# Graph attention: self-loops added to the sums by VectorE from rows by head and node, and the one-hot scaling folded into the weights

## The chip, the cores and the metric

The kernel runs on one core of a Trainium2 chip. The metric is the device time of one execution in microseconds (us). The median of three runs is shown beside the lowest and the highest. One more execution was taken by the hardware profiler, and every row of the profile comes from that one.

## The reference, cut to what matters

Four graph layers follow each other on 6,250 nodes with 128 features and 106,250 edges. The edges are sorted by destination. The change touches only the fourth layer, an attention with H = 3 heads in which each node also attends to itself over a "loop" edge:

```
row2 = concat([row, loop]); col2 = concat([col, loop])
ea2  = concat([edge_attr, loop_attr])          # loop_attr: mean of the node's edge attributes
alpha = a_src[row2] + a_dst[col2] + a_edge
alpha = where(alpha >= 0, alpha, 0.2 * alpha)
m = segment_max(alpha, col2)
ex = exp(alpha - m[col2])
denom = segment_sum(ex, col2)
attn = ex / denom[col2]
agg = segment_sum(attn[:, :, None] * xp[row2], col2)
y = agg.reshape(n, H * OUT) @ lin_W + lin_b
return layernorm(x + y) * ln_g + ln_b
```

So for each node and head there is a maximum over the logits of the node's edges and of its own loop, then a sum of exponentials, and a sum of source rows weighted by them.

## The kernel before, in words

**The stages ahead of it.** Sums of edge features, a graph convolution and two more neighbour sums fill the first 2,310 us of the span. The last of them, in the function `then` (L1000 to L1032), normalises the node features x, and writes one row of XW = 136 numbers for each node to the DRAM table x3: 128 features, 3 source logits, the number 1, 3 loop logits, and padding. ScalarE's queue sends these rows (L1032), and a memset on GpSimd sets the ones (L1006).

**The attention loop.** The edges are cut into 208 blocks of 512 (BT = 4 tiles of 128 edges). Because edges are sorted, the destinations of a block lie in a window of BW = 40 nodes; where it starts is held in a table, from which SyncE and VectorE load registers, four blocks at a time (`bases`, L296 to L310). The last tile of the block before also counts as one, so that a node whose edges cross a block's border is whole. With the loops, S = BT + 2 = 6 tiles are worked on for each block: the tile carried over, four own tiles, and a tile of the window's nodes, one node in a row, for the loops. A stage `relb` (L146 to L152) holds for each edge the position of its destination in the window; the loops' column in it is simply the row number (L151).

Three functions do the work of a block b:

- `weigh(b)` (L1082 to L1118): GpSimd gathers four tiles of source rows from x3 (L1087), SyncE loads the window's 128 rows for the loops (L1093). VectorE makes logits z for the four own tiles (L1095, then `lrelu`, L312), ScalarE copies the loops' logits (L1097) and those of the tile carried over (L1099). VectorE compares positions with 0 to 39 (L1103: a one-hot of 128 x 6 x 40), turns 1 and 0 into 0 and -1e30 (L1108), and adds z for the three heads (L1110: 128 x 720). TensorE transposes the six parts, each 128 x 120, into PSUM (L1115), and VectorE takes the maximum over all edges (L1118): one number for each of 120 pairs of head and node.
- `power(b)` (L1120 to L1127): TensorE transposes the maxima back, copied over 128 rows (L1122), VectorE subtracts them (L1125), ScalarE takes the exponential (L1127).
- `gather(b)` (L1129 to L1143): six fp32 matmuls sum the rows and the ones, weighted (L1136: 120 x 132; each is two records in the profile, while a transpose is one). VectorE takes the reciprocal of the denominator (L1138), ScalarE scales (L1140), TensorE transposes (L1142), and VectorE copies the result to its window in `acc` (L1143).

**What sets the order.** The loop at the function's end calls power(b - 1), gather(b - 2) and weigh(b), and after every 16 blocks or so `end` (L1064 to L1080), which multiplies `acc` with the output weights (L1069) and does two layernorms. A scheduler then orders the instructions of each engine ahead of time; each engine works through its own queue in that order. Waits are on semaphores. Pools set how far work runs ahead: 8 buffers of gathered rows, 5 of loop rows, 4 of z, 3 each of one-hots and weights, 2 PSUM tiles of two banks each for the transposes, 2 for the sums.

```python
        for b in range(NBT + 2):
            if 1 <= b <= NBT:
                power(b - 1)
            if b >= 2:
                gather(b - 2)
            if b < NBT:
                weigh(b)
```

Of the kernel before, what the change touches and what calls it, by code (L numbers as in the profile page):

```python
# [8 lines left out]
F32 = mybir.dt.float32  # L9
I32 = mybir.dt.int32  # L10
AF = mybir.ActivationFunctionType
OP = mybir.AluOpType
AX = mybir.AxisListType
# [6 lines left out]
F = 128  # L20
# [5 lines left out]
H = 3  # L26
EPS = 1e-5
LOW = -1e30
# [12 lines left out]
BT, NBT, BW = 4, 208, 40  # L41
PB, NB5 = 125, 50
# [8 lines left out]
XW = 136  # L51
# [3 lines left out]
def gnn_kernel(ctx: ExitStack, tc: tile.TileContext, a: dict, out: bass.AP):  # L55
    nc = tc.nc
    const = ctx.enter_context(tc.tile_pool(name="base", bufs=1))
# [4 lines left out]
    part = const.tile([128, 1], F32, name="part")  # L62
# [15 lines left out]
        "relb": const.tile([128, NBT, BT + 2], F32, name="relb"),  # L78
# [4 lines left out]
    with tc.tile_pool(name="ix", bufs=1) as sp, \  # L83
# [51 lines left out]
        for c in range(0, NT, 417):  # L135
            w = min(417, NT - c)
# [14 lines left out]
        nc.vector.tensor_copy(relb[:, :, BT + 1:BT + 2].rearrange("p g j -> p (g j)"),  # L151
                              part.to_broadcast([128, NBT]))  # L152
# [49 lines left out]
def by_windows(ctx: ExitStack, tc: tile.TileContext, a: dict, out: bass.AP, consts, ix):  # L202


    nc = tc.nc
# [785 lines left out]
    with tc.tile_pool(name="l2bw", bufs=2) as work, \  # L991
# [8 lines left out]
        def then(k):  # L1000
# [5 lines left out]
            nc.gpsimd.memset(xw[:, :, F + H:XW], 1.0)  # L1006
# [13 lines left out]
            nc.vector.tensor_copy(xw[:PB, :nb, F:F + H], ap[:PB, :nb, 0:H])  # L1020
# [5 lines left out]
            nc.vector.tensor_add(lg, lg, xw[:PB, :nb, F:F + H])  # L1026
# [24 lines left out]
    S = BT + 2  # L1051
    with tc.tile_pool(name="gb", bufs=8) as gp, tc.tile_pool(name="lr", bufs=5) as lrp, \
# [29 lines left out]
        def weigh(b):  # L1082
# [9 lines left out]
            loop = loops_[b] = lrp.tile([128, XW], F32, name="loop")  # L1092
            nc.sync.dma_start(loop, x3[ds(of_sp(b), 128), :])  # L1093
            z = zs[b] = zbp.tile([128, S, H], F32, name="z")
            nc.vector.tensor_add(z[:, 1:1 + BT, :], r[:, :, F:F + H], zed[:, BT * b:BT * (b + 1), :])  # L1095
            lrelu(z[:, 1:1 + BT, :].rearrange("p j h -> p (j h)"))
            nc.scalar.copy(z[:, S - 1, :], loop[:, F + H + 1:F + 2 * H + 1])  # L1097
            if b:
                nc.scalar.copy(z[:, 0, :], zs.pop(b - 1)[:, BT, :])  # L1099
            else:  # L1100
# [5 lines left out]
                                    op=OP.is_equal)  # L1106

            nc.vector.tensor_scalar(oh, oh, -1.0, -LOW, op0=OP.add, op1=OP.mult)  # L1108
            w = ws[b] = wbp.tile([128, S, H, BW], F32, name="w3")
            nc.vector.tensor_tensor(w, oh.to_broadcast([128, S, H, BW]),  # L1110
                                    z.rearrange("p j (h w) -> p j h w", w=1).to_broadcast([128, S, H, BW]),
                                    op=OP.add)
            tp = tps.tile([H * BW, 2, 512], F32, name="w_p")
            for j in range(S):
                nc.tensor.transpose(tp[:, j // 3, j % 3 * 128:(j % 3 + 1) * 128],  # L1115
                                    w[:, j, :, :].rearrange("p h w -> p (h w)"), ident)
            mx = ms[b] = zbp.tile([H * BW, 1], F32, name="mx")
            nc.vector.tensor_reduce(mx, tp[:, :, 0:384], AX.XY, OP.max)  # L1118

        def power(b):  # L1120
            mb = both[:, b % 2]
            nc.tensor.transpose(mb.rearrange("p h w -> p (h w)"), ms.pop(b).to_broadcast([H * BW, 128]),  # L1122
                                ident[:H * BW, :H * BW])
            wf = ws[b].rearrange("p j h w -> p j (h w)")
            nc.vector.tensor_tensor(wf, wf, mb.rearrange("p (j h) w -> p j (h w)", j=1)  # L1125
                                    .to_broadcast([128, S, H * BW]), op=OP.subtract)
            nc.scalar.activation(wf, wf, AF.Exp)  # L1127

        def gather(b):  # L1129
            wf = ws.pop(b).rearrange("p j h w -> p j (h w)")  # L1130
            loop = loops_.pop(b)
            r0 = rows.pop(b - 1)[:, BT - 1, 0:F + H + 1] if b else loop[:, 0:F + H + 1]
            o = ops.tile([H * BW, F + H + 1], F32, name="o")
            for j in range(S):
                rr = r0 if j == 0 else loop[:, 0:F + H + 1] if j == S - 1 else rows[b][:, j - 1, 0:F + H + 1]
                nc.tensor.matmul(o, lhsT=wf[:, j, :], rhs=rr, start=(j == 0), stop=(j == S - 1))  # L1136
            rd = zbp.tile([H * BW, 1], F32, name="rd")
            nc.vector.reciprocal(rd, o[:, F + H:F + H + 1])  # L1138
            on = obp.tile([H * BW, F], F32, name="on")
            nc.scalar.activation(on, o[:, 0:F], AF.Copy, scale=rd)  # L1140
# [707 lines left out]
```

## Time and profile before

| what | value |
|---|---|
| median of three runs | 3670.23 us (3645.24 to 3673.68) |
| the profiled execution's own time | 3699.71 us |
| its span, first to last instruction | 3697.9 us, 43585 instructions |
| first loop row load (the attention loop begins) | 2309.97 us |
| attention loop to the end of the span | 1388 us, 6.67 us for each of 208 blocks |
| TensorE, matmuls busy over the span | 2650.3 us (72%) |
| VectorE busy | 1841.0 us (50%) |
| ScalarE busy | 911.8 us (25%) |
| GpSimd busy | 1651.7 us (45%) |
| mean granted TensorE clock | 0.803 of full |

A row of instruction groups has the line, the engine, the operation, what it writes and reads with shapes, how often, the busy time and the mean of one in ns, and then the idle time of the engine just ahead of these instructions with what ended it. PE is TensorE, PEld its weight load, DVE VectorE, ACT ScalarE, POOL GpSimd, and a name with a q at its end is that engine's sequencer. A matmul's end is modelled, not measured. "issue" and "remote" name waits for which no instruction is seen that ended them.

### The profile page before, as it was taken

What the parts mean: (1) busy time and instruction counts of PE and PEld (TensorE: products, weight loads), DVE (VectorE), ACT (ScalarE), POOL (GpSimd) and SP (SyncE); (2) the same over time, 40 slices, a digit from 0 to 9 for tenths busy, and PEclk for the clock granted to TensorE, in tenths of its full rate; (3) what the DMA queues carried; (4) which work ended last, traced back from release to release, by engine and by line L of the source; (5) the groups of instructions that cost most, each with busy time, mean ns of one, the idle gap of its engine ahead of it and who ended that gap; (6) DMA issues with size and microseconds to landing.
All of it is one profiled execution on the core that took longest, in us unless ns stands there. A gap on an engine that the chain in (4) does not pass through costs nothing.

```text
span 3697.9 us, 43585 instructions
## 1 busy us (share of the span) xinstructions
PE 2650.3 (72%) x14544; PEld 1631.1 (44%) x14544; DVE 1841.0 (50%) x6113; ACT 911.8 (25%) x1657; POOL 1651.7 (45%) x1684
## 2 busy tenths in 40 slices
PE   2787879776689859999787894465556666555665
PEld 1334436332234424445333442355555555545555
DVE  4899975455522630000211123465666666566666
ACT  0677764200000510001100010122222222222222
POOL 3000010366660575440555521665656656665662
PEclk6677779798889979999887996677777767777777
DMA  5588851465555346653554562222222222222221
GB/s 156 177 280 274 281 195 48 124 194 160 159 168 177 79 116 195 199 181 113 160 170 144 174 173 69 58 53 57 58 58 56 59 57 56 54 59 55 57 56 34
DMA packets 333524, 461.85 MB, mean 125 GB/s; under 512 B 43998, under 2 KB 217854, under 8 KB 332933
## 3 DMA queue, kind: packets, MB, share of 16 engines
q1 hardware_dynamic: 250754, 278.98, 25.5%
q0 software_dynamic: 54912, 105.86, 11.6%
q10 hardware_dynamic: 27624, 74.14, 5.4%
q8 instruction: 117, 1.92, 0.2%
q14 instruction: 117, 0.96, 0.1%
HBM read 375.30 MB, written 83.36 MB: 124 GB/s over the span
## 4 chain that ended last, share of the span: by engine, by line
PE 42%; issue 12%; DVE 11%; another core or an unknown queue 5%; DMA 3%; POOL 2%; ACT 2%; DVEq 1%; SPq 0%; ACTq 0%; POOLq 0%
PE sums L812 21%; PE o L1136 10%; PE w_p L1115 4%; DVE w L1125 2%; DVE w L1110 1%; POOL row L767 1%; PE both L320 1%; PE yp L981 1%; ACT w L1127 1%; DVE mx L1118 1%; PE both L1122 1%; PE fp L1069 1%; PE hp L869 1%; PE both L1142 1%
## 5 line engine op out<-in xcount | busy, mean ns | idle before, releaser
L812 PE MATMUL sums<-piece,arena 125*128 125x500 bf16 x4500 | 1051.3, 387 | 61.1 <-issue 47.2
L1087 POOL DMA_INDIRECT rows<-x,srca x831 | 821.0, 988 | 552.6 <-issue 212.1
L767 POOL DMA_INDIRECT row<-table,srca x549 | 540.0, 984 | 436.0 <-issue 138.8
L812 PEld LDWEIGHTS <-arena 125*128 125x128 bf16 x4500 | 439.1, 99 | 610.9 <-issue 148.8
L1136 PE MATMUL o<-rows,w 128*120 128x132 f32 x2078 | 446.1, 368 | 252.0 <-issue 137.4
L1136 PEld LDWEIGHTS o<-rows,w 128*120 128x120 f32 x2078 | 382.9, 258 | 297.5 <-issue 167.5
L614 ACT CAST arena<-made 128x1000 bf16<-128x1000 f32 (+1 forms) x260 | 312.8, 1261 | 63.6 <-PE made L612 55.3
L611 DVE TENSOR_SCALAR okey<-iok,key 128x250 bf16<-128x250 bf16 x1000 | 314.5, 314 | 0.0
L1115 PE MATMUL w_p<-ident,w 128*120 128x128 f32 x1248 | 246.0, 341 | 92.7 <-DVE w L1110 45.7
L1127 ACT ACTIVATE w<-w 128x720 f32<-128x720 f32 x208 | 167.0, 803 | 532.5 <-DVE w L1125 380.9
L612 PE MATMUL made<-okey,olow 128*128 128x250 bf16 x1000 | 249.7, 331 | 61.7 <-ACT arena L614 27.5
L609 DVE TENSOR_SCALAR olow<-iob,low 128x128 bf16<-128x128 bf16 x1000 | 279.6, 280 | 0.0
L1125 DVE TENSOR_TENSOR w<-w,both 128x720 f32<-128x720 f32 x208 | 187.5, 901 | 178.7 <-remote 106.3
L1118 DVE TENSOR_REDUCE mx<-w_p 120x1 f32<-120x768 f32 x208 | 198.2, 954 | 156.1 <-PE o L1136 85.9
L1115 PEld LDWEIGHTS w_p<-ident,w 128*120 128x120 f32 x1248 | 198.0, 177 | 112.1 <-issue 89.1
L322 ACT COPY by_node<-both 128x128 f32<-128x128 f32 (+1 forms) x48 | 12.7, 264 | 896.1 <-PE both L320 630.8
L331 DVE TENSOR_TENSOR onehot<-iota,relg 128x384 f32<-128x384 f32 x118 | 65.9, 561 | 258.5 <-remote 115.2
L612 PEld LDWEIGHTS <-olow 128*128 128x128 bf16 x1000 | 108.6, 114 | 184.9 <-DVE okey L611 87.3
L1110 DVE TENSOR_TENSOR w<-oh,z 128x720 f32<-128x720 f32 x208 | 186.8, 898 | 0.2
L683 POOL MEMSET ea<- 128x128 f32 x1 | 0.2, 228 | 397.5 <-PE sums L320 397.5
L320 PE MATMUL both<-row,onehot 128*32 128x128 f32 x1098 | 65.6, 312 | 141.3 <-DVE arena L327 94.0
L1142 PE MATMUL both<-ident,on 120*128 120x120 f32 x208 | 71.6, 344 | 111.8 <-DVE w L1125 85.7
(283 smaller groups left out, 3196.2 us busy)
## 6 DMA issues: line engine op xcount, KB each, us to landing
piece<-edges SPq DMA_DIRECT2D x300, 625.0 KB
edges<-arena ACTq DMA_DIRECT2D x100, 625.0 KB
ea<-in_edge_attr_dram SPq DMA_DIRECT2D x69, 768.0 KB
loop<-x SPq DMA_DIRECT2D x208, 68.0 KB
rows<-x,srca POOLq DMA_INDIRECT x831
row<-table,srca POOLq DMA_INDIRECT x549
eat<-in_edge_attr_dram POOLq DMA_DIRECT2D x28, 236.0 KB
table<-xn SPq DMA_DIRECT2D x24, 250.0 KB
```

The source lines that it names most:

```text
L609: nc.vector.tensor_scalar(o, iob, low[:, g:g + 1], None, op0=OP.is_equal)
L611: nc.vector.tensor_scalar(w, iok, key[:, g:g + 1], None, op0=OP.is_equal)
L612: nc.tensor.matmul(p[:, i, 0:NB5 * GD], lhsT=o, rhs=w, start=True, stop=True)
L614: nc.scalar.copy(to, p[:, 0:n, 0:NB5 * GD].rearrange("p i (h d) -> p i h d", d=GD))
L767: nc.gpsimd.indirect_dma_start(out=r[:, j, :], out_offset=None, in_=table, in_offset=bass.IndirectOffsetOnAxis(ap=ix["src"][:, t:t + 1], a ...
L812: nc.tensor.matmul(p, lhsT=xp[:PB, h, i, :], rhs=t[:PB, :, (h - h0) * SC:(h - h0 + 1) * SC], start=(h == 0 and i == 0), stop=(h == NB5 - 1 ...
L1087: nc.gpsimd.indirect_dma_start(out=r[:, j, :], out_offset=None, in_=x3, in_offset=bass.IndirectOffsetOnAxis(ap=ix["src"][:, BT * b + j:BT ...
L1110: nc.vector.tensor_tensor(w, oh.to_broadcast([128, S, H, BW]), z.rearrange("p j (h w) -> p j h w", w=1).to_broadcast([128, S, H, BW]), op= ...
L1115: nc.tensor.transpose(tp[:, j // 3, j % 3 * 128:(j % 3 + 1) * 128], w[:, j, :, :].rearrange("p h w -> p (h w)"), ident)
L1118: nc.vector.tensor_reduce(mx, tp[:, :, 0:384], AX.XY, OP.max)
L1125: nc.vector.tensor_tensor(wf, wf, mb.rearrange("p (j h) w -> p j (h w)", j=1) .to_broadcast([128, S, H * BW]), op=OP.subtract)
L1136: nc.tensor.matmul(o, lhsT=wf[:, j, :], rhs=rr, start=(j == 0), stop=(j == S - 1))
```

## The change: what it does

The loops no longer have a tile of their own among the edges: S falls from 6 to 5. Instead a tile `loop` of 120 rows, one for each pair of head and node, is loaded: for each head the 40 window rows, features and the number 1 (129 columns), and beside them that head's loop logit (one column). So six loads take the place of one. ScalarE copies the logit column into the PSUM tile of the transposes as one more column, so that the maximum holds it. The maximum is stored negated. ScalarE also takes exp(logit - maximum) of the loops, and after the matmuls VectorE adds loop weight x loop row to the sums, with the number 1 carrying the denominator. The columns of x3 are reordered (128 features, 1, 3 source logits, 3 loop logits), which takes three columns off the matmuls. The comparison is turned round to "not equal" and the scaling by -1e30 happens in the instruction that adds z, which is one per head.

```diff
-        "relb": const.tile([128, NBT, BT + 2], F32, name="relb"),
+        "relb": const.tile([128, NBT, BT + 1], F32, name="relb"),
...
-        nc.vector.tensor_copy(relb[:, :, BT + 1:BT + 2].rearrange("p g j -> p (g j)"),
-                              part.to_broadcast([128, NBT]))
...
-            nc.gpsimd.memset(xw[:, :, F + H:XW], 1.0)
+            nc.gpsimd.memset(xw[:, :, F:XW], 1.0)
...
-            nc.vector.tensor_copy(xw[:PB, :nb, F:F + H], ap[:PB, :nb, 0:H])
+            nc.vector.tensor_copy(xw[:PB, :nb, F + 1:F + H + 1], ap[:PB, :nb, 0:H])
...
-    S = BT + 2
+    S = BT + 1
...
-            loop = loops_[b] = lrp.tile([128, XW], F32, name="loop")
-            nc.sync.dma_start(loop, x3[ds(of_sp(b), 128), :])
+            loop = loops_[b] = lrp.tile([H * BW, F + 2], F32, name="loop")
+            at = of_sp(b)
+            for h in range(H):
+                hs = slice(h * BW, (h + 1) * BW)
+                nc.sync.dma_start(loop[hs, 0:F + 1], x3[ds(at, BW), 0:F + 1])
+                nc.sync.dma_start(loop[hs, F + 1:F + 2], x3[ds(at, BW), F + 1 + H + h:F + 2 + H + h])
...
-            nc.scalar.copy(z[:, S - 1, :], loop[:, F + H + 1:F + 2 * H + 1])
...
-                                    op=OP.is_equal)
-
-            nc.vector.tensor_scalar(oh, oh, -1.0, -LOW, op0=OP.add, op1=OP.mult)
+                                    op=OP.not_equal)
+
             w = ws[b] = wbp.tile([128, S, H, BW], F32, name="w3")
-            nc.vector.tensor_tensor(w, oh.to_broadcast([128, S, H, BW]),
-                                    z.rearrange("p j (h w) -> p j h w", w=1).to_broadcast([128, S, H, BW]),
-                                    op=OP.add)
-            tp = tps.tile([H * BW, 2, 512], F32, name="w_p")
+            for h in range(H):
+                nc.vector.scalar_tensor_tensor(w[:, :, h, :], oh[:, :, 0, :], LOW,
+                                               z[:, :, h:h + 1].to_broadcast([128, S, BW]), op0=OP.mult, op1=OP.add)
+            tp = tps.tile([H * BW, 1024], F32, name="w_p")
...
+            nc.scalar.copy(tp[:, S * 128:S * 128 + 1], loop[:, F + 1:F + 2])
             mx = ms[b] = zbp.tile([H * BW, 1], F32, name="mx")
-            nc.vector.tensor_reduce(mx, tp[:, :, 0:384], AX.XY, OP.max)
+            nc.vector.tensor_reduce(mx, tp[:, 0:S * 128 + 1], AX.X, OP.max, negate=True)
...
-                                    .to_broadcast([128, S, H * BW]), op=OP.subtract)
+                                    .to_broadcast([128, S, H * BW]), op=OP.add)
             nc.scalar.activation(wf, wf, AF.Exp)
+            loop = loops_[b][:, F + 1:F + 2]
+            nc.scalar.activation(loop, loop, AF.Exp, bias=ms.pop(b))
...
-            o = ops.tile([H * BW, F + H + 1], F32, name="o")
+            o = ops.tile([H * BW, F + 1], F32, name="o")
             for j in range(S):
-                rr = r0 if j == 0 else loop[:, 0:F + H + 1] if j == S - 1 else rows[b][:, j - 1, 0:F + H + 1]
-                nc.tensor.matmul(o, lhsT=wf[:, j, :], rhs=rr, start=(j == 0), stop=(j == S - 1))
+                nc.tensor.matmul(o, lhsT=wf[:, j, :], rhs=rows[b][:, j - 1, 0:F + 1] if j else r0,
+                                 start=(j == 0), stop=(j == S - 1))
+
+            nc.vector.scalar_tensor_tensor(loop[:, 0:F + 1], loop[:, 0:F + 1], loop[:, F + 1:F + 2], o,
+                                           op0=OP.mult, op1=OP.add)
             rd = zbp.tile([H * BW, 1], F32, name="rd")
-            nc.vector.reciprocal(rd, o[:, F + H:F + H + 1])
+            nc.vector.reciprocal(rd, loop[:, F:F + 1])
             on = obp.tile([H * BW, F], F32, name="on")
-            nc.scalar.activation(on, o[:, 0:F], AF.Copy, scale=rd)
+            nc.scalar.activation(on, loop[:, 0:F], AF.Copy, scale=rd)
```

## The prediction

> **What bounds the kernel now.** I read the page first, then busy time by stretches, the groups by shape in the attention loop, the chain of waits there, and the timeline of single blocks. The change alters only the attention loop, which begins with the first loop load at 2309.97 us and fills the remaining 1388 us: 6.67 us for each of 208 blocks. Everything ahead keeps its order (a memset of eight columns for five, and one copy of 0.36 us on VectorE, L151, fall outside and are left out of the sum). The busy time of that stretch (length, then PE, PEld, DVE, ACT and POOL with counts, clock, DMA share, GB/s):
>
> ```profile
> 2310.00:3698.00 1388.00, 823.08 (x4460) 727.08 (x4460) 855.46 (x2265) 365.38 (x907) 820.99 (x831) 0.72 0.23 55
> ```
>
> No engine is over 62% and DMA is at 0.23, so neither a single engine's sum nor bandwidth sets the end. The groups by shape:
>
> ```profile
> L1087 POOL DMA_INDIRECT rows<-x,srca x800 | 791.2, 989 | 507.7 <-issue 203.0 <-PE o L1136 162.2 <-DVE w L1110 79.1
> L1136 PE MATMUL o<-rows,w 128*120 128x132 f32 x2066 | 443.5, 368 | 252.0 <-issue 137.4 <-ACT w L1127 111.5 <-remote 0.3
> L1115 PE MATMUL w_p<-ident,w 128*120 128x128 f32 x1230 | 241.3, 340 | 80.3 <-DVE w L1110 42.0 <-issue 24.3 <-DVE rstd L277 8.3
> L1118 DVE TENSOR_REDUCE mx<-w_p 120x1 f32<-120x768 f32 x206 | 196.3, 954 | 156.1 <-PE o L1136 85.9 <-PE w_p L1115 46.0 <-remote 19.5
> L1125 DVE TENSOR_TENSOR w<-w,both 128x720 f32<-128x720 f32 x206 | 185.7, 902 | 178.7 <-remote 106.3 <-PE w_p L1115 37.8 <-PE both L1122 29.8
> L1110 DVE TENSOR_TENSOR w<-oh,z 128x720 f32<-128x720 f32 x205 | 184.1, 898 | 0.0
> L1127 ACT ACTIVATE w<-w 128x720 f32<-128x720 f32 x206 | 165.4, 803 | 531.4 <-DVE w L1125 380.9 <-issue 106.5 <-DVE rd L1138 23.3
> L1103 DVE TENSOR_TENSOR oh<-iota,relb 128x240 f32<-128x240 f32 x202 | 81.0, 401 | 0.0
> L1108 DVE TENSOR_SCALAR oh<-oh 128x240 f32<-128x240 f32 x202 | 61.8, 306 | 0.0
> ```
>
> VectorE's idle time lies ahead of the maximum and the subtraction, and TensorE ends it. ScalarE waits for VectorE, TensorE for ScalarE: a ring. GpSimd needs 0.94 us and 0.30 us of issue for each gather, so 4 x 1.24 = 5.0 us for a block: a floor of 1030 us, 350 us below. The chain of waits from 2400 to 3600 us names TensorE (the line ends where the answer ends it):
>
> ```profile
> by line: PE o L1136 26.9%; issue 22.4%; PE w_p L1115 9.9%; another core or an unknown queue 8.8%; DVE w L1125 4.3%; DVE w L1110 3.9%; ACT w L1127 3.3%; PE both L1122 2.5%; DVE mx L1118 2.4%; PE fp L1069 2.2%; PE both L1142 1.6%; DVE oh L110
> ```
>
> What "issue" and the unknown queue hide shows in the timeline of two blocks:
>
> ```profile
> 2933.14 1.45 PE L1115 MATMUL w_p<-ident,w 128*120 128x128 f32 x6
> 2934.64 0.96 DVE L1118 TENSOR_REDUCE mx<-w_p 120x1 f32<-120x768 f32 x1 [0.70 <-PE w_p L1115]
> ...
> 2937.04 0.82 PE L1115 MATMUL w_p<-ident,w 128*120 128x128 f32 x6
> ...
> 2942.59 0.96 DVE L1118 TENSOR_REDUCE mx<-w_p 120x1 f32<-120x768 f32 x1 [2.72 <-PE o L1136]
> ```
>
> The first maximum starts 0.05 us after its six transposes, recorded at the half clock; the second 4.7 us after transposes recorded at the full clock, though VectorE stood idle for 2.7 us. So in stretches with the full clock TensorE is later than its records say. In all 208 blocks: where VectorE idled ahead of the subtraction, it began 0.45 us (median, 87 cases) after the start of the transpose that it needs if that ran at the half clock, 2.6 us (51 cases) if at the full. I therefore count these two shares as TensorE's: 26.9 + 9.9 + 2.5 + 2.2 + 1.6 + 22.4 + 8.8 = 74%.
>
> [...] the first loop load, issued at 2309.97, lets ScalarE go at 2311.92, 1.95 us.
>
> **The change part by part.**
>
> TensorE, per block: one transpose goes (0.21 us from start to start at the half clock: six in 1.45 us, the last lasting 0.42) and two records of L1136 (0.22 each, from single starts in the timeline); 129 columns for 132 save 0.05 over ten. Together 0.70 us, 146 us in 208 blocks if TensorE sets every block; by its share of the chain, 0.74 x 146 = 108 us.
>
> VectorE, per block: L1108 goes (0.306). [...] L1110: three fused instructions of 200 elements at 0.37 = 1.10 for 0.90; [...] Subtraction 720 to 600: 0.78 for 0.90. New fused addition of 129: 0.29, as the PSUM copy L1143 (120 elements, 0.278). Sum 3.46 before, 3.36 after: -0.10 us; -0.26 if each instruction overlaps the next by 0.08 us as the timeline shows (two more instructions). VectorE holds some 12% of the chain: 5 us. [...]
>
> ScalarE: exponential over 600: 0.803 - 120 x (0.803 - 0.189)/717 = 0.70, so -0.10 between subtraction and sums. TensorE's wait for it ends 65 of 208 blocks' sums: 7 us. The copy of loop logits (0.19) becomes a copy into PSUM; a small exponential is added (0.2 to 0.3, by the nearest row, L1140, 0.356 for 128). ScalarE has room at 26%, but see the order below.
>
> Gains: 108 + 5 + 7 = 120 us.
>
> Waits added. (a) In the built kernel's order every one of the 208 copies into the transposes' tile waits for TensorE, and the maximum then waits for ScalarE: one engine more. Price 0.2 for the copy and 0.1 for the second hand-over. The maximum found VectorE idle in 115 of 208 blocks: 35 us. Bounds: 0 (the maximum is due only at the end of the sums of the block before, 10 x 0.22 = 2.2 us later, which hides 0.3 + 0.82) and 62 us. (b) Queued behind that copy: in 113 of 206 blocks the copy of block b + 1 stands ahead of the exponential of b on ScalarE. The copy ends five transposes later (0.2 + 1.07 + 0.25 + 0.2 = 1.7 us after the maxima's transpose started), the subtraction after 0.45 + 0.78 = 1.2. So the exponential is 0.45 us late, and behind it the sums. A third of the blocks (65 of 208 above): 113 x 0.45 / 3 = 17 us; bounds 0 and, if TensorE stands still for 1.0 us each time, 113. (c) Between sums and scaling lies the fused addition. Where the transpose of the scaled result stands ahead of the next block's sums (78 blocks, 41 before), TensorE waits for it: 37 x (0.29 + some 0.06 of waiting on its loads' semaphores) = 13 us; bounds 0 and 37 x 1.0.
>
> Loads: six for one. SyncE spends 0.53 us on each (issues at 2309.97, 2310.53, 2311.07), with registers every fourth block 0.23 more: 3.4 of 6.4 us. A loop buffer now comes free when the scaling is done, and its copy is due at least two blocks, some 12 us, later: 3.4 + 2 us fit. Past them SyncE issues only the output store after each layernorm, queued with them as before. If the cover went (SyncE over 6 us a block), each block would gain the excess. The loads' 4-byte pieces (120 a block) burden DMA at 0.24 little. The row gathers, GpSimd's instructions and their queue stay.
>
> Costs 35 + 17 + 13 = 65. Net -120 + 65 = -55 us: own time 3699.7 to 3645, or against the median of 3670.23, which is 29 us below the profiled execution, 3615 us.
>
> **The rivals.**
>
> TensorE sets nearly everything. For: 74% of the chain, and waits (a) to (c) lie under its work. Then the whole 146 us come, with a little from VectorE: -150, 3520 us. Against: in half-clock blocks TensorE now has five transposes (1.07) between the maxima and the sums instead of 0.44 + 1.28, less than the 2.1 us which subtraction and exponential need (0.45 + 0.78 + 0.70 + hand-overs), so it stands idle for what it saved.
>
> Nothing moves: this idling takes it all. At the half clock a block costs 0.2 + 0.44 + 1.28 + 0.3 idle + 2.2 + 0.2 = 4.6 us before; after, 2.1 to 2.5 + 2.16 + 0.2 = 4.5 to 4.9. Result 3660 us, within 1%.
>
> Slower: the copy holds the exponential (b). The ring is then transposes, copy, exponential, sums, one after another, with TensorE idle for 0.25 + 0.2 + 0.7 + 0.1 = 1.25 us in 113 blocks and where it was 0.3 before: +0.95 x 113 = 107, with (a) at 62 and (c) at 22, against gains of 120: +70, 3740 us. It decides once the added waits exceed 120/208 = 0.58 us a block.
>
> That the change does not do what it says is excluded: the built order has five transposes and five sums a block.
>
> **How the numbers follow.** Forecast (3615; own range 3575 to 3650) 0.37, TensorE sets all 0.25, nothing moves 0.16, slower 0.22. Single runs differ by 0.8%, so about 1%, 37 us, is what a measurement can tell from no change. Faster by more: 0.25 + 0.75 of 0.37 = 0.53; within: 0.25 x 0.37 + 0.16, less a little, = 0.24; slower 0.23. The range, 3500 to 3735, leaves out a larger gain (0.07) and the worse half of the slower case.
>
> **What would show it.** Right: L1115's and L1136's successors at 1040 and 2080 records; the maximum near 0.82 us, released by ScalarE; the subtraction 0.78, exponential 0.70; no wait for loop loads over 2 us. Step (b) shows as idle time of the sums behind the exponential, and of the exponential behind the copy. Wrong: a chain led by SyncE or DMA, or TensorE's share unchanged at an unchanged time; or GpSimd's waits for buffers gone, so that gathers bound the loop.

## The result and the profile after

The changed kernel takes 3805.15 us (median of 4 runs, 3796.49 to 3810.95) where the kernel before took 3671.95 beside it: a ratio of 1.0375, 95% interval 1.0318 to 1.0431. It is slower by 133 us, above the predicted range, where the forecast of 3615 was a gain. The profiled execution took 3796.49 us with a span of 3794.6; the one of the kernel before had taken 3699.71, so the two profiles lie 97 us apart and not 133.

The attention stage by itself: length, then busy time of PE, PEld, DVE, ACT and POOL with counts, granted clock, DMA share, GB/s.

```profile
2310.00:3795.00 1485.00, 793.10 (x3836) 691.93 (x3836) 809.69 (x2676) 395.88 (x1115) 798.07 (x827) 0.63 0.24 51
```

Against the row of before (1388 us) the stage is 97 us longer: it holds the whole difference of the two profiles. This is so though TensorE has 624 records fewer and VectorE 46 us less busy time. The busy time did go; what grew is idle time. The granted clock fell from 0.72 to 0.63, and TensorE's busy time fell by 30 us only. The clock's records in both traces are at 1.0 or at 0.5, the full and the half clock: full for 44% of the stage before, for 26% here. The groups of the stage (busy us, mean ns of one, then idle time ahead of them and what ended it):

```profile
L1085 POOL DMA_INDIRECT rows<-x,srca x827 | 798.2, 965 | 627.8 <-issue 228.5 <-PE o L1138 142.4 <-DVE w L1112 138.1
L1138 PE MATMUL o<-rows,w 128*120 128x129 f32 x2080 | 472.1, 394 | 346.3 <-ACT w L1128 291.1 <-issue 47.7 <-ACT w_p L1117 7.4
L1116 PE MATMUL w_p<-ident,w 128*120 128x128 f32 x1040 | 240.1, 372 | 161.9 <-DVE z L310 66.7 <-DVE w L1112 28.7 <-issue 20.4
L1112 DVE SCALAR_TENSOR_TENSOR w<-oh,z 128x200 f32<-128x200 f32 x624 | 200.9, 356 | 0.2
L1119 DVE TENSOR_REDUCE mx<-w_p 120x1 f32<-120x641 f32 x208 | 169.8, 818 | 85.4 <-ACT w_p L1117 73.0 <-issue 10.5
L1126 DVE TENSOR_TENSOR w<-w,both 128x600 f32<-128x600 f32 x208 | 161.7, 778 | 182.2 <-remote 98.5 <-PE both L1123 30.6 <-PE w_p L1116 19.6
L1128 ACT ACTIVATE w<-w 128x600 f32<-128x600 f32 x208 | 145.8, 701 | 253.9 <-DVE w L1126 176.9 <-issue 70.4 <-DVE oh L1105 3.8
L1141 DVE SCALAR_TENSOR_TENSOR loop<-loop,o 120x129 f32<-120x129 f32 x208 | 72.3, 347 | 240.5 <-remote 115.8 <-PE o L1138 49.0 <-issue 35.7
L1117 ACT COPY w_p<-loop 120x1 f32<-120x1 f32 x208 | 33.8, 163 | 573.1 <-remote 320.1 <-PE w_p L1116 188.3 <-PE o L1138 24.3
```

The durations are what the prediction said (818 for 0.82, 778 for 0.78, 701 for 0.70; only the fused addition is dearer, 0.35 for 0.29). VectorE's follow from rows of before, too: 401 ns for 240 elements and 898 for 720 are 1.04 ns an element, and with that as an estimate the maximum comes to 0.82 us (from 954 ns for 768) and the subtraction to 0.78 (from 902 for 720). The waits are not. TensorE stands idle for 346 us ahead of the sums (252 before) and for 162 ahead of the transposes (80). ScalarE waits 573 us in front of the copy L1117, and the exponential L1128 comes behind it. "remote" means that no instruction was recorded as ending shortly before the wait ended. In this stage every such wait ended at an update of one semaphore, and in the trace only TensorE's matmuls count that one up: 125 waits with 579 us here, 71 with 192 in the kernel before. So they are waits for TensorE. Some lines of the timeline show it:

```profile
3004.07 0.71 PE L1116 MATMUL w_p<-ident,w 128*120 128x128 f32 x5
...
3007.66 0.78 DVE L1126 TENSOR_TENSOR w<-w,both 128x600 f32<-128x600 f32 x1 [3.53 <-remote]
...
3009.71 0.70 SPq L1095 DMA_DIRECT2D loop<-x  x1
...
3010.56 0.16 ACT L1117 COPY w_p<-loop 120x1 f32<-120x1 f32 x1 [7.48 <-remote]
3010.66 0.70 ACT L1128 ACTIVATE w<-w 128x600 f32<-128x600 f32 x1
3010.76 0.82 DVE L1119 TENSOR_REDUCE mx<-w_p 120x1 f32<-120x641 f32 x1 [2.05 <-ACT w_p L1117]
3011.41 2.19 PEld L1138 LDWEIGHTS o<-rows,w 128*120 128x120 f32 x10 [6.88 <-ACT w L1128]
```

The transposes are recorded as done at 3004.8, the copy that needs them starts at 3010.6: TensorE is 5.8 us later than its records. The subtraction ended at 3008.44, its exponential waits 2.2 us more behind that copy, and the sums stand behind it. It looks like the slower rival, "the copy holds the exponential". The experiments say that the picture is true, and that taking the copy out of the way does not bring the loss back.

### The profile page after: what moved, and what is told of

It reads as the page before. It is cut to its first block, busy times and chain, and to the rows that moved or that the text cites. A ratio compares the mean times of both kernels' runs of the same rounds, so it can differ in the third digit from the quotient of the medians.

```text
span 3794.6 us, 47107 instructions
## 1 busy us (share of the span) xinstructions
PE 2620.5 (69%) x13920; PEld 1599.7 (42%) x13920; DVE 1796.1 (47%) x6528; ACT 943.2 (25%) x1865; POOL 1633.1 (43%) x1684
## 5 line engine op out<-in xcount | busy, mean ns | idle before, releaser
L1138 PE MATMUL o<-rows,w 128*120 128x129 f32 x2080 | 472.1, 394 | 346.3 <-ACT w L1128 291.1
L1138 PEld LDWEIGHTS o<-rows,w 128*120 128x120 f32 x2080 | 417.6, 286 | 385.3 <-ACT w L1128 313.1
L609 DVE TENSOR_SCALAR okey<-iok,key 128x250 bf16<-128x250 bf16 x1000 | 285.6, 286 | 0.0
L607 DVE TENSOR_SCALAR olow<-iob,low 128x128 bf16<-128x128 bf16 x1000 | 250.9, 251 | 0.0
L1126 DVE TENSOR_TENSOR w<-w,both 128x600 f32<-128x600 f32 x208 | 161.7, 778 | 182.2 <-remote 98.5
L1119 DVE TENSOR_REDUCE mx<-w_p 120x1 f32<-120x641 f32 x208 | 169.8, 818 | 85.4 <-ACT w_p L1117 73.0
L1128 ACT ACTIVATE w<-w 128x600 f32<-128x600 f32 x208 | 145.8, 701 | 253.9 <-DVE w L1126 176.9
L1112 DVE SCALAR_TENSOR_TENSOR w<-oh,z 128x200 f32<-128x200 f32 x624 | 200.9, 356 | 0.2
L1141 DVE SCALAR_TENSOR_TENSOR loop<-loop,o 120x129 f32<-120x129 f32 x208 | 72.3, 347 | 240.5 <-remote 115.8
L1117 ACT COPY w_p<-loop 120x1 f32<-120x1 f32 x208 | 33.8, 163 | 573.1 <-remote 320.1
```

The lines of the kernel that those rows point to most:

```text
L607: nc.vector.tensor_scalar(o, iob, low[:, g:g + 1], None, op0=OP.is_equal)
L609: nc.vector.tensor_scalar(w, iok, key[:, g:g + 1], None, op0=OP.is_equal)
L1112: nc.vector.scalar_tensor_tensor(w[:, :, h, :], oh[:, :, 0, :], LOW, z[:, :, h:h + 1].to_broadcast([128, S, BW]), op0=OP.mult, op1=OP.add)
L1119: nc.vector.tensor_reduce(mx, tp[:, 0:S * 128 + 1], AX.X, OP.max, negate=True)
L1138: nc.tensor.matmul(o, lhsT=wf[:, j, :], rhs=rows[b][:, j - 1, 0:F + 1] if j else r0, start=(j == 0), stop=(j == S - 1))
```

## The experiments

The runs fall into five series, each on one chip with the kernel before beside it; times are compared inside a series or by their ratio to before. In the second of them before took 3409 us and not 3667 to 3699; the last section comes back to that.

**First series (before 3699.09).** Four parts of the change, each undone alone. The changed kernel itself did not run in this series; beside before it stood at 1.0375 in the result above, and at 1.041 and 1.0314 in the third and fourth series. The scheduler gave the first three of these kernels another order of instructions than the changed kernel has, so each differs from it in more than its edit. All kernels that only load the loops in another way (two loads, and one and three further down) keep its order on TensorE, VectorE and ScalarE. The copy taken away:

```diff
-            nc.scalar.copy(tp[:, S * 128:S * 128 + 1], loop[:, F + 1:F + 2])
...
-            nc.vector.tensor_reduce(mx, tp[:, 0:S * 128 + 1], AX.X, OP.max, negate=True)
+            nc.vector.tensor_reduce(mx, tp[:, 0:S * 128], AX.X, OP.max, negate=True)
+            nc.vector.scalar_tensor_tensor(mx, loop[:, F + 1:F + 2], -1.0, mx, op0=OP.mult, op1=OP.min)
```

> The changed kernel without ScalarE's copy into the transposes' tile (L1117): the maximum reads the 640 transposed columns, and one more tiny fused instruction on VectorE takes the smaller of it and the negated loop logit. Theory A (the hop TensorE to ScalarE to VectorE sets the loss: the copy waits for the transposes, the maximum for the copy, and the exponential of the block before stands queued behind the copy): the 573 us that the copy waits leave ScalarE's queue, the 254 us that the exponential waits and the 346 us that the sums wait shrink, and the time falls from 3805 by 100 us or more, to 3600 to 3700. Theory B (the six loads on SyncE) and theory C (three fused additions in place of one, on VectorE): within 40 us of 3805, or up to 40 above, since VectorE gets 0.16 to 0.2 us a block more (208 x 0.2 = 40).

Measured: 3838.47, ratio 1.0357 (1.0298 to 1.0417). The gain of 100 us or more that theory A asked for is not there. The wait in front of the sums stays without any copy in the way (groups of this kernel):

```profile
L1138 PE MATMUL o<-rows,w 128*120 128x129 f32 x2080 | 461.7, 380 | 371.3 <-ACT w L1128 283.1 <-issue 88.0
L1128 ACT ACTIVATE w<-w 128x600 f32<-128x600 f32 x208 | 146.2, 703 | 581.6 <-DVE w L1126 374.5 <-issue 137.6 <-DVE rd L1144 37.1
```

The 254 us that the exponential waited have become 582: of the 573 us that the copy had waited, 328 now stand in front of the instruction behind it, which waits for the subtraction. So most of the wait was for something earlier and not for the copy. A smaller gain may be hidden by the other order.

The copy moved ahead of the transposes:

```diff
+            nc.scalar.copy(tp[:, S * 128:S * 128 + 1], loop[:, F + 1:F + 2])
             for j in range(S):
...
-            nc.scalar.copy(tp[:, S * 128:S * 128 + 1], loop[:, F + 1:F + 2])
```

> The changed kernel with ScalarE's copy issued ahead of the five transposes: it waits only for the buffer and the loop's logits, so it is short of the transposes, and the maximum waits for TensorE again. The copy still stands in the queues, so this takes away its wait and not its work. Theory A: like the kernel without the copy, 3600 to 3700, if the buffer comes free early; where the copy then waits for the maximum that frees the buffer, and the transposes wait for the copy, part of it stays, 3700 to 3760. Theories B and C: 3805 within 30 us.

Measured: 3833.26, 1.034 (1.0289 to 1.0392). The copy's own wait fell from 573 to 20 us and the time did not follow.

The fold undone:

```diff
-                                    op=OP.not_equal)
-            for h in range(H):
-                nc.vector.scalar_tensor_tensor(w[:, :, h, :], oh[:, :, 0, :], LOW, ...
+                                    op=OP.is_equal)
+            nc.vector.tensor_scalar(oh, oh, -1.0, -LOW, op0=OP.add, op1=OP.mult)
+            nc.vector.tensor_tensor(w, oh.to_broadcast([128, S, H, BW]), ...
```

> The changed kernel with the scaling of one-hots and the one addition over all heads put back (is_equal, scaling, addition) for the three fused instructions. VectorE's busy time for it: 3 x 0.356 = 1.07 us against about 0.27 + 0.78 = 1.05, so as much. Theory C (the three fused instructions cost what their busy time does not show): it falls by 60 us or more, to below 3745. Theories A and B: 3805 within 30 us.

Measured: 3835.3, 1.0336 (1.0287 to 1.0384). Undoing the fold does not give the 60 us that theory C asked for.

Two loads for six:

```diff
-            for h in range(H):
-                hs = slice(h * BW, (h + 1) * BW)
-                nc.sync.dma_start(loop[hs, 0:F + 1], x3[ds(at, BW), 0:F + 1])
-                nc.sync.dma_start(loop[hs, F + 1:F + 2], x3[ds(at, BW), F + 1 + H + h:F + 2 + H + h])
+            nc.sync.dma_start(loop[:, 0:F + 1], x3[ds(at, BW), 0:F + 1].rearrange("(h w) f -> h w f", h=1)
+                              .to_broadcast([H, BW, F + 1]))
+            nc.sync.dma_start(loop[:, F + 1:F + 2], x3[ds(at, BW), F + 1 + H:F + 1 + 2 * H]
+                              .rearrange("w (h f) -> h w f", f=1))
```

> The changed kernel with two loop loads a block instead of six: all heads in one access pattern. SyncE issues 2 x 0.53 = 1.1 us a block instead of 3.2. Theory B (SyncE's issue or its loads are late and hold the buffers, the fused addition or the copy): it falls by 60 us or more, to below 3745; the 24 plus 37 us that copy and fused addition are seen to wait for loads are the least of that, so 3745 to 3780 would be B in that size alone. Theories A and C: 3805 within 25 us.

Measured: 3850.86, 1.0397 (1.0351 to 1.0442). Fewer load instructions alone gain nothing. The number of pieces (unbroken parts of rows, 240 a block) was still the same here, and SyncE's recorded time for the loads hardly shrank: 0.73 us (median) for each of two, where each of the six has 0.29.

**Second series (before 3409.19).** The fold alone in the kernel before (the fold's diff above, turned round, with six tiles), the loops left out, one load, and TensorE's work put back. The loops left out (with their loads and the small exponential):

```diff
-            nc.scalar.copy(tp[:, S * 128:S * 128 + 1], loop[:, F + 1:F + 2])
...
-            nc.vector.scalar_tensor_tensor(loop[:, 0:F + 1], loop[:, 0:F + 1], loop[:, F + 1:F + 2], o, ...
...
-            nc.vector.reciprocal(rd, loop[:, F:F + 1])
+            nc.vector.reciprocal(rd, o[:, F:F + 1])
```

One load:

```diff
-            loop = loops_[b] = lrp.tile([H * BW, F + 2], F32, name="loop")
...
+            loop = loops_[b] = lrp.tile([128, F + 2], F32, name="loop")
+            nc.sync.dma_start(loop, x3[ds(of_sp(b), 128), 0:F + 2])
+            loop = loops_[b] = loop[0:H * BW, :]
```

The sixth tile:

```diff
+            nc.tensor.transpose(tp[:, 768:896], w[:, 0, :, :].rearrange("p h w -> p (h w)"), ident)
...
-            for j in range(S):
-                nc.tensor.matmul(o, lhsT=wf[:, j, :], rhs=rows[b][:, j - 1, 0:F + 1] if j else r0,
+            for j in range(S + 1):
+                nc.tensor.matmul(o, lhsT=wf[:, j % S, :], rhs=rows[b][:, j % S - 1, 0:F + 1] if j % S else r0,
```

> The kernel before with the folding alone: not_equal and three fused additions of 240 elements (estimate 0.40 us each, from 0.356 at 200) in place of is_equal, scaling (0.306) and one addition (0.898). VectorE gets 1.20 us for 1.20, so nothing by busy time. Four undone parts of the change (the copy, its place, the fold, the number of loads) each left the changed kernel within 20 us of itself, so the loss should lie in what is left: theory D (the loops' addition and exponential as new links in the ring) or E (TensorE with a tile less runs at the half clock more). Both expect here no change, within 30 us of before. Theory C (the fused three cost more than their busy time): 30 to 100 us slower than before.

> The changed kernel with the loops left out of the computation (no loop loads, no copy, no small exponential, no fused addition; sums and denominators lack each node's own row). It keeps five transposes, five sums and the fold. Theory D, B or any other that puts the loss into the new links or loads: it falls far below before, by the 120 us of gains and perhaps more, to 3500 to 3600 where before is 3672. Theory E (a shorter TensorE part alone makes the blocks no faster, since the half clock is then granted more often): above 3700, near the changed kernel.

> The changed kernel with one loop load of 128 consecutive rows in place of six (the rows for the second and third head then belong to the wrong nodes, and all take the first head's logit: what is added is another node's row). It takes SyncE's instructions and the 120 four-byte pieces back to about what they were before; copy, exponential and addition stay. The kernel with two loads kept all 240 pieces, and stayed as slow. Theory B' (the pieces and the long SyncE stream slow the stage, not the number of loads): 60 to 150 us below the changed kernel. Theories D and E: within 25 us of it.

> The changed kernel with the sixth transpose and a sixth pair of sums put back as work without use (the first tile is transposed and summed twice, so its rows count double). TensorE does about 0.70 us a block more. If TensorE's time sets the end: 108 to 146 us above the changed kernel, some 3920 to 3950. If TensorE is not what sets the end (theories B and D): within 40 us of it. Theory E (TensorE slowed because less work lowers its clock): clock back to 0.72 in the stage and faster than the changed kernel, toward 3700 to 3780.

Measured: the fold alone 3339.1 (0.9789, 0.9773 to 0.9806), no loops 3336.03 (0.9785, 0.9769 to 0.9801), one load 3345.69 (0.981, 0.9794 to 0.9827), six tiles 3403.42 (0.9981, 0.9964 to 0.9998). The series could not be set against the others, since the kernel before was itself some 260 us faster in it. What it does show: here the fold alone gains 70 us, and leaving the loops out altogether, on top of the fold, gains nothing more. The stage then takes 1119 us for 831 gathers that need 1.24 us each, 1030 us: in this series the gathers are near.

**Third series (before 3694.2).** The changed kernel again, with two of these beside it.

> The changed kernel itself once more, beside its relatives. The kernels without loops, with one load, with six tiles and with the fold alone ran on a chip on which the kernel before takes 3409 us, not 3672, and there none of SyncE's register instructions took over 0.6 us, while in the profile of the changed kernel 272 did. Theory F (the loss belongs to chips on which TensorE and SyncE go through stretches of such slow steps, and the change is a gain without them): on a chip with before near 3409, 0.98 to 0.995 of before, below the 3403 of the kernel with six tiles; on a chip with before near 3670 to 3700, 1.03 to 1.045 again. Theory D (the new links of the ring, on any chip): 1.03 or more on both.

> The kernel without loops again (it leaves each node's own row out of sums and denominators). On a chip with before near 3409: 0.9785 again. On a chip with before near 3690: theory F with the slow steps caused by SyncE's many instructions or the loads' pieces says 0.94 to 0.98, since there are neither; theory E' (there a stage with less TensorE work is slow by itself) says 1.00 or more.

> The changed kernel with one load of 128 consecutive rows again (heads 2 and 3 get other nodes' rows). On a chip with before near 3409: 0.981 again. On a chip with before near 3690: if SyncE's instructions and the pieces bring the slow steps, 0.96 to 1.00, well below the changed kernel beside it; if they don't, 1.03 like it.

Measured: the changed kernel 3849.41 (1.041, 1.0363 to 1.0457), no loops 3710.43 (1.0042, 1.0025 to 1.0059), one load 3754.83 (1.0158, 1.0113 to 1.0203). So of the 139 us between loops left out and the full change, 44 come with copy, small exponential, fused addition and one load (and with another order of instructions), and 95 with six loads in place of one. The two kernels that differ only in the loads have the same order of instructions on the other engines, so their waits can be set side by side. The changed kernel in this series:

```profile
L1126 DVE TENSOR_TENSOR w<-w,both 128x600 f32<-128x600 f32 x208 | 161.8, 778 | 175.4 <-remote 89.2 <-PE both L1123 33.2 <-issue 29.2
L1141 DVE SCALAR_TENSOR_TENSOR loop<-loop,o 120x129 f32<-120x129 f32 x208 | 72.4, 348 | 296.2 <-remote 159.1 <-PE o L1138 49.6 <-issue 46.9
L1117 ACT COPY w_p<-loop 120x1 f32<-120x1 f32 x208 | 33.8, 163 | 592.1 <-remote 341.3 <-PE w_p L1116 181.4 <-PE o L1138 32.2
```

With one load (its lines are three lower):

```profile
L1123 DVE TENSOR_TENSOR w<-w,both 128x600 f32<-128x600 f32 x208 | 161.7, 777 | 141.9 <-PE both L1120 51.4 <-remote 42.3 <-PE w_p L1113 40.5
L1138 DVE SCALAR_TENSOR_TENSOR loop<-loop,o 120x129 f32<-120x129 f32 x208 | 72.0, 346 | 212.2 <-remote 106.7 <-PE o L1135 47.9 <-issue 22.8
L1114 ACT COPY w_p<-loop 120x1 f32<-120x1 f32 x208 | 33.8, 163 | 496.9 <-remote 251.3 <-PE w_p L1113 202.8 <-PE o L1135 21.6
```

All three wait for TensorE, by the code and by the semaphore that ended the "remote" waits; these fall from 590 to 400 us. Waits of these instructions for the loads themselves are small in both (44 us in 24 waits with six, none with one). So the loads seldom arrive late: with more of them TensorE is late.

**Fourth series (before 3674.24).**

> The changed kernel once more, as the measure for its relatives on the same chip. On a chip with before near 3690: 1.03 to 1.045 of before, as twice. On one with before near 3409, where it has not run: 0.985 to 1.00 if its loss belongs to the slow steps of TensorE and SyncE, since there the kernel with one load took 0.981 and that with a sixth tile 0.998; over 1.03 if the loss is the same on every chip.

> The kernel before with the fold alone. It took 0.979 of before on the chip with 3409. On a chip near 3690: undoing the fold in the changed kernel moved nothing there (3835 against about 3840), so 0.99 to 1.01; if the fold's shorter way (one instruction less between z and transposes) counts in every case, 0.98.

The loads of single logits left out:

```diff
-                nc.sync.dma_start(loop[hs, 0:F + 1], x3[ds(at, BW), 0:F + 1])
-                nc.sync.dma_start(loop[hs, F + 1:F + 2], x3[ds(at, BW), F + 1 + H + h:F + 2 + H + h])
+                nc.sync.dma_start(loop[h * BW:(h + 1) * BW, :], x3[ds(at, BW), 0:F + 2])
```

> The changed kernel with three loads of 130 columns, one a head, and without the three loads of single logits (column F+1 is then the first head's source score, so the loop's weight is a wrong number). SyncE issues half, and of 240 pieces a block the 120 of 4 bytes are gone. If the 4-byte pieces cost the 94 us between six loads (1.041) and one load (1.016) on the slower chips: near 1.016. If the number of SyncE's instructions or of pieces as such does: about half way, 1.028. If the way of loading rows by head does: 1.04. On the chip with 3409: at or below the changed kernel, 0.98.

> The changed kernel with a sixth transpose and a sixth pair of sums as work without use (the first tile counts double), now on the chip it falls on. On a chip near 3690: leaving the loops out there gave no gain at all (1.004), so TensorE's 0.70 us a block should not set the end, within 25 us of the changed kernel beside it; 108 us or more above it if it does. On the chip with 3409 again 0.998, and the distance from the changed kernel there is then the price of TensorE's work on that chip.

Measured: the changed kernel 3799.47 (1.0314, 1.028 to 1.0347), the fold alone 3653.18 (0.9946, 0.9927 to 0.9965), three loads 3761.06 (1.0235, 1.0196 to 1.0274), six tiles 3767.24 (1.0242, 1.0211 to 1.0274). The three loads of single logits, with their 120 pieces of 4 bytes a block, cost 38 us, in one series and at one order. The rest of the 95 would lie between one load of 128 rows and three of 40; these two ran in different series. The fold alone is a gain of 21 us (it has one instruction more than before, not less as its expectation says). And the kernel with more TensorE work is 32 us faster than the one without. Their stages, the changed kernel and then the one with six tiles:

```profile
2313.00:3811.00 1498.00, 789.64 (x3837) 689.90 (x3836) 811.39 (x2681) 395.63 (x1115) 798.10 (x831) 0.63 0.21 50
```

```profile
2308.00:3760.00 1452.00, 809.68 (x4460) 725.20 (x4460) 811.72 (x2681) 404.91 (x1115) 803.90 (x831) 0.72 0.22 52
```

For the gain there are two readings: the clock (0.72, and 0.63 without the added work), or the order of instructions, since the scheduler places them anew for each kernel: the transpose of the scaled rows stands ahead of the next sums in 78 blocks of the changed kernel, and in 12 of this one. The fifth series tells them apart.

**Fifth series (before 3667.54).** One order for all three kernels: the changed one, the same with the filler of the sixth tile (diff above), and before with the fold. The order is made by an edge from each instruction to the one before it on its engine:

```diff
+        def q(i):
+            i = i.ins
+            if i.engine in last:
+                tc.add_manual_dep(i, last[i.engine], mybir.DependencyInfo(
+                    mybir.DependencyClass.NoSync, mybir.DependencyReason.DATA), reason="order")
+            last[i.engine] = i.name
...
+            if b < NBT:
+                weigh(b)
+            if b >= 2:
+                sums(b - 2)
             if 1 <= b <= NBT:
+                maxima(b - 1)
                 power(b - 1)
+            if b < NBT:
+                turn(b)
             if b >= 2:
-                gather(b - 2)
+                scale(b - 2)
             if b < NBT:
-                weigh(b)
+                top(b)
+            if b >= 2:
+                turned(b - 2)
```

> The changed kernel with a fixed order of its attention instructions on TensorE, VectorE and ScalarE, the same in every block: weights of block b, sums of b - 2, maxima's transpose, subtraction and exponential of b - 1, transposes of b, addition and scaling of b - 2, copy and maximum of b, transpose of the scaled rows. The copy of b then always stands behind the exponential of b - 1. Theory O (the loss comes with the order in which the built program puts the instructions, which differs in every variant): falls from 1.03 to 1.04 of before to 1.00 or less. Theories of the new links, the pieces and the clock: 1.02 to 1.04, with more waiting where the order is stiffer.

> The same fixed order with a sixth transpose and a sixth pair of sums as work without use (the first tile counts double): it differs from the one before in nothing but TensorE's work, some 0.70 us a block at the half clock. Theory E (TensorE loses the full clock when its work shrinks, and that costs more than the work): 0.5% or more faster than the ordered changed kernel. Theory O: equal, or slower by up to 0.7 x 208 = 146 us (4%).

> The kernel before with the fold and the same fixed order: loops as a sixth tile of TensorE, one load a block, no copy into the transposes' tile, no small exponential, no fused addition. Against the ordered changed kernel this is the exchange of the loops alone at one order. If the exchange is a loss by itself (links, pieces): this one is 2 to 4% faster than that. If the loss is one of order: equal, or up to 2% slower. Against before (without order, 0.9946 with the fold alone) it shows what the order is worth.

Measured: the changed kernel 3733.85 (1.0193, 1.0132 to 1.0253), with the filler 3777.25 (1.0289, 1.0232 to 1.0346), before with the fold 3681.8 (1.0032, 1.0014 to 1.0051). The stages (columns as above), of the changed kernel in the fixed order:

```profile
2310.00:3726.00 1416.00, 804.41 (x3836) 657.07 (x3836) 857.12 (x2681) 330.51 (x1091) 800.93 (x831) 0.64 0.25 53
```

with TensorE's filler:

```profile
2302.00:3774.00 1472.00, 822.43 (x4460) 705.10 (x4460) 855.98 (x2681) 329.62 (x1091) 795.84 (x831) 0.73 0.24 51
```

and of before with fold and fixed order:

```profile
2320.00:3687.00 1367.00, 812.12 (x4460) 702.79 (x4460) 877.01 (x2473) 328.66 (x907) 808.04 (x831) 0.74 0.24 56
```

The filler adds 624 records and the clock rises from 0.64 to 0.73, as it does in the fourth series; yet the time rises too, by 43 us (the two intervals just overlap, but each of the four runs with the filler is slower than each of the four without). Theory E, that the change loses by its lower clock, does not hold at this order: the clock rose with the work. The lower one eats part of what was saved: a record of the sums lasts 387 ns on average without the filler and 352 with it, and 624 more records add only 18 us of busy time. So the gain of 32 us in the fourth series most likely came with the order, the other thing that changed there. What a better order takes away is TensorE's lateness: the changed kernel's "remote" waits are 128 us in 34 waits here, against 579 to 623 us in its three profiles with the built order. And third against first: at one and the same order, exchanging the sixth tile for the loops' own rows costs 52 us.

## Why the prediction was wrong

**The sum, as measured.** In the fourth series the changed kernel stands 125 us above before: the fold gives -21, the exchange of the loops +146. At the fixed order the exchange is +52. The other 94 (76, if the ratios are subtracted) go with the order that the built program gets: the fixed order makes the changed kernel faster (1.0314 to 1.0193) and before with the fold slower (0.9946 to 1.0032). Only one fixed order was tried, and another would split the sum differently. In the 52 there is TensorE's saving, -43, so loads and new links cost 95 at this order; that six loads in place of one also cost 95, at the built order, does not show that the new links cost nothing.

**"TensorE ... by its share of the chain, 0.74 x 146 = 108 us."** This step failed. The work is there and removable, but at a fixed order, where it was put back, it is worth 43 us, 0.30 of 146, not 0.74. I had added the chain's "issue" and "unknown queue" to TensorE's share, because VectorE began late after transposes recorded at the full clock. The lateness is TensorE's, but it is not made of the records that I removed: with 624 records fewer, "remote" waits grew from 192 to 579 us, and the subtraction's own stayed (106.3 us before, 98.5 after). The share that sums and transposes have themselves in the chain, 26.9 + 9.9 = 37%, would have given 54 us. Part of the saving is lost with the lower clock as well (0.64, and 0.73 with the filler): the filler's 624 records add 18 us of busy time only.

**The loads: "3.4 + 2 us fit", and "The loads' 4-byte pieces (120 a block) burden DMA at 0.24 little."** The sum has no term for the loads, and this step failed as well. It costs most of what was measured inside one order of instructions: 95 us for six loads of 240 pieces in place of one of 128, and 38 of the same kind for the three loads of 4-byte pieces alone. The cover that I named did its work: the loads are hardly waited for (44 us in 24 waits). What I left out is that loads in time may still make another engine late (590 us of waits for TensorE with six loads, 400 with one). What in the six loads does it is shown in part only. Two loads with 240 pieces were no better than six, so it is not their number by itself (that kernel ran in another series than its measure, but in the same order of instructions). Nor is it the number of pieces by itself, since three loads with 120 pieces stand at 1.0235 and one with 128 at 1.0158, again in two series. The transfers of instructions that the profile counts do not follow the time either: 155 on queue 14 with six loads, 128 with two, 122 with one. SyncE shows a slowness of its own: 278 of its register instructions took over 0.5 us in the changed kernel, 14 before, 35 with one load, 72 with two; the time does not go with their number. By which way the loads make TensorE late is open; no run here separates it.

**(a) and (b), the hop through ScalarE and the exponential behind the copy, 52 us.** Neither taking the copy away nor moving it showed a gain (1.0357 and 1.034, where the change itself is at 1.0314 to 1.041). Both kernels got another order, which can hide a gain or a loss of tens of us. At the fixed order, where the copy stands behind the exponential in every block, (b) cannot occur, so it may be part of what the fixed order gains for the changed kernel; the 52 us are lost without it. And (a) is visible there: the maximum waits 232 us for the copy, and 281 in all, 184 in the kernel without it. How much of these 97 us lies on the path was not separated from the loads.

**(c) and the order, 13 us.** The prediction counted one pair of instructions, from the built order, and priced it. The scheduler moved many more, and the order as a whole was worth 76 to 94 us of the difference. Which pairs matter was not found.

**VectorE, -5 us.** The fold is worth -21 (0.9946): right in sign, too small in size. The fused additions of the changed kernel take 0.356 us each, where 0.37 was my estimate and the rows of before (1.04 ns an element from 401 ns for 240) give 0.36 for 200 elements; since the kernel with the fold alone has an order of its own too, the rest may be that, and at the fixed order it was not tried against before.

**The rivals.** The side of the slower one was right; its mechanism, the copy holding the exponential, is seen in the trace, but no run shows that it decided. "Nothing moves" came nearest for the saving alone: leaving the loops out altogether, with the whole saving and none of the new links, came to 1.0042. Whether by the idling that this rival named, or by its own order, was not shown.

**A version that beats both.** The fold alone in the kernel before: 0.9946 of before in the fourth series (0.9927 to 0.9965), 0.9789 in the second (0.9773 to 0.9806).

## What to carry to other kernels

An engine that is waited for need not be one whose instructions are too long (here the waits for TensorE grew from 192 to 579 us with 624 records fewer): price removed work by its own share of the chain, without what the chain calls "issue" or unknown (here 54 us for 43 measured). Do not put small transfers at nothing because nobody waits for them: here they cost 95 us, with 44 us of waits. Where a scheduler places the instructions, a variant can also be another order; one fixed order for all variants tells what an edit is worth at that order.

## What the runs showed of the hardware that was not expected

One program ran 12% apart in two series: the kernel with one load took 3345.69 us where before took 3409, and 3754.83 where before took 3694. Its stage in the faster series, and then in the slower:

```profile
2216.00:3347.00 1131.00, 658.97 (x3836) 567.35 (x3836) 804.46 (x2681) 394.74 (x1115) 807.18 (x831) 0.77 0.29 67
```

```profile
2320.00:3752.00 1432.00, 769.99 (x3837) 670.16 (x3836) 811.01 (x2681) 393.98 (x1115) 797.18 (x831) 0.65 0.21 53
```

VectorE, ScalarE and GpSimd have the same busy time within 1.3%; TensorE has 111 us more at a lower clock, and the stage is 301 us longer. In the faster series none of SyncE's register instructions took over 0.5 us, in the slower 35; not even the kernel with six loads and six tiles had one in the faster series, in some 2,500. The faster series has no "remote" wait in this stage, in none of its four kernels; with one load the slower one has 111, with 466 us. Where a reader of TensorE's results had to wait, it began 0.04 us (median) after the recorded end of the last record that it needs: at the half clock in both series, and at the full clock in the faster one. At the full clock in the slower series it began 0.65 us (the copy), 0.68 us (the fused addition) and 1.24 us (the subtraction) after it. So the stretches in which TensorE is later than its records belong to the slower series and its full clock.

The price of a change depends on it: copy, small exponential, fused addition and one load together cost 10 us in the faster series and 44 in the slower. The changed kernel itself did not run in the faster series; whether it loses there is open. What makes a series fast is open too: the second and the fourth bear the same chip number, 0, and before took 3409 us in one and 3674 in the other.
